# A fill on GpSimd behind each group's gathers, and node inputs loaded at a quad's sums, in a graph attention layer on one Trainium2 core

## The chip, the core and the metric

The kernel runs on 1 core of a Trainium2 chip. A core has a matrix engine (TensorE, PE in the profile; its weight loads are PEld), a vector engine (VectorE, DVE), a scalar engine (ScalarE, ACT), a general engine (GpSimd, POOL) and a sequencer that mostly issues transfers (SyncE, SP). Each takes its own instructions in order; they wait for each other through semaphores. Transfers run on 16 DMA engines.

The metric is device time in microseconds (us). Beside the timed runs, one execution was taken by the hardware profiler; all views of the profile are of that one.

## The reference, cut to what matters

One layer of graph attention over 12500 nodes of 128 features and 200000 edges, sorted by destination. The input is normalised and rectified, projected to 4 heads of 32, scored per edge, put through a softmax over each destination's edges, and summed.

```
h = maximum(layernorm(x), 0)                       # 12500 x 128
hn = (h @ W_node.T).reshape(N, 4, 32)
e  = (edge_attr_64 @ W_edge.T).reshape(E, 4, 32)
att = sum(concat([hn[src], hn[dst], e], -1) * a, -1)     # per edge and head
att = where(att > 0, att, 0.2 * att)
m = maximum(segment_max(att, dst), 0)
ex = exp(att - m[dst])
denom = segment_sum(ex, dst) + (E - deg)[:, None] * exp(-m)
out = x + segment_sum((ex / denom[dst])[:, :, None] * hn[src], dst).reshape(N, 128)
```

The node input `x` is needed twice: at the start, for the projection, and at the end, where it is added to the sums.

## The kernel before, in words

**Tiling.** Edges go in groups of 511 (one more place of the 512 carries the sum of a destination that goes on from the group before). There are 392 groups; 4 groups are a quad (98 quads), and 4 quads, 16 groups, are in most places a "super", the unit of the softmax. Since edges are sorted, a group's destinations lie in a window of at most 92 rows (`SPAN`).

**Stages.** First all nodes are normalised and projected (lines 307 to 448) and written to a table in device memory, 137 numbers a node. Then, for each quad: *logits* (`all_logits`, `open_logits`, `logits`, `add_sources`), for each super the *softmax*, and for each quad the *sums* (`sums`, `complete_group`, `divide`). Sums of one super run beside the logits of the next.

**Gathers.** The rows of the edges' sources are fetched by GpSimd: `gather` (line 132) issues, for each group, four indirect transfers (line 141), 128 rows each, into `ga`. The first 18 groups gather raw rows of `x` before the table is there (72 transfers), the others gather from the table (1494). `ga` has room for 8 quads (`QUADS`). A quad's gathers are issued by `fetch`, which `open_logits(q)` calls for quad q + 2; the first gather of each group waits until PE has summed the group that lay in that place before, eight quads back.

**SyncE's queue.** `open_logits(q)` also issues, for quad q + 2: the edge features `ea` (line 302), the destinations `db` (line 304, waits for a free buffer), and in `fetch_windows` four loads of `pw` (line 502) and four of the node inputs `xw` (line 505, 92 rows of 512 bytes each). A register load on SP precedes each four (`windows`, line 486). Between these stand the stores of the results, four a quad (line 783), which `divide` issues.

**Sums.** For each group DVE weighs the gathered rows (line 736) and makes a matrix of ones and zeros (`hot`, line 749); PE multiplies them for three of the four parts (line 754). The part j = 0 waits for the group before: DVE line 683 and ACT line 687 carry its last row over, PE line 688 multiplies, ACT line 689 copies the sums out (`pt`). A quad's division comes one group later: DVE lines 766 to 776 and the addition of `xw` at line 780 (on GpSimd for a few at the end).

**Order.** The order of instructions on each engine is the program's own: within `tc.manual_schedule()` nothing is reordered, and `together` takes one step of each of its generators in turn. Where a quad's sums and another's logits go together, `sums(q)` comes first, so that its first instructions stand ahead of the loads that `open_logits` issues.

Of the kernel before, what the change touches and what calls it, by code (L numbers as in the profile page):

```python
# [8 lines left out]
F32 = mybir.dt.float32  # L9
# [9 lines left out]
D = H * HD  # L19
# [10 lines left out]
WIN = 96  # L30
SPAN = 92
QG = 4
# [2 lines left out]
SIDE = PIECES * H  # L35
NODE_T = 9
AT_ONCE = 4
RAW, MORE = 4, 2
QUADS = 8
SETS = max(NODE_T, QG * J)  # L40
# [3 lines left out]
def blocks(total, step):  # L44
    return [(i, min(step, total - i)) for i in range(0, total, step)]
# [3 lines left out]
def kernel(  # L49
# [35 lines left out]
    nc = tc.nc  # L85
# [5 lines left out]
    consts = ctx.enter_context(tc.tile_pool(name="consts", bufs=1))  # L91
# [14 lines left out]
                   allow_small_or_imprecise_dtypes=True)  # L106
    ones = consts.tile([P, P], F32, name="ones")
    nc.vector.memset(ones, 1.0)

# [10 lines left out]
    quads = blocks(G, QG)  # L122
# [9 lines left out]
    def gather(q, rows, width, lo, hi):  # L132

        g0, m = quads[q]
        ga = GA[q] = ga_all[:, q % QUADS]
        for i in range(lo, hi):
            n = -(-min(E - (g0 + i) * NE + 1, GE) // P)
            if n < J:
                nc.vector.memset(ga[:, i, n:, :], 0.0)
            for j in range(n):  # L140
                nc.gpsimd.indirect_dma_start(  # L141
                    out=ga[:, i, j, 0:width], out_offset=None, in_=rows,
                    in_offset=bass.IndirectOffsetOnAxis(ap=srci[:, g0 + i, j:j + 1], axis=0))

    def held_gather(q, i, rows, width):

        nc.vector.memset(ga_all[0:1, q % QUADS, i, 0, 0:1], 0.0)
        gather(q, rows, width, i, i + 1)
# [8 lines left out]
    with tc.manual_schedule():  # L157
# [5 lines left out]
        early = [(q, i) for q in range(raw + 1) for i in range(raws(q))]  # L163
        for _ in range(AT_ONCE):
            q, i = early.pop(0)
            gather(q, x, D, i, i + 1)
# [11 lines left out]
        with tc.tile_pool(name="prep", bufs=1) as prep, tc.tile_pool(  # L178
            name="prep_ps", bufs=1, space=bass.MemoryType.PSUM
# [127 lines left out]
        with tc.tile_pool(name="node", bufs=2) as node, tc.tile_pool(  # L307
            name="node_ps", bufs=2, space=bass.MemoryType.PSUM
        ) as node_ps, tc.tile_pool(name="index", bufs=1) as index, tc.tile_pool(
            name="index_ps", bufs=1, space=bass.MemoryType.PSUM  # L310
# [152 lines left out]
    with tc.tile_pool(name="work", bufs=2) as work, \  # L463
            tc.tile_pool(name="turned", bufs=1) as turned, \
            tc.tile_pool(name="ps", bufs=1, space=bass.MemoryType.PSUM) as ps:
        XW, LG, AT, U, DR = {}, {}, {}, {}, {}
# [10 lines left out]
        def groups(s):  # L477
            q0, m = supers[s]
            g0 = quads[q0][0]
            return g0, quads[q0 + m - 1][0] + quads[q0 + m - 1][1] - g0  # L480
# [3 lines left out]
        def windows(of, size, g, n):  # L484

            return nc.values_load_multi_w_load_instructions(
                of[0:1, g:g + n], engines=[mybir.EngineType.SP], min_val=0, max_val=(N - 1) * size,
                skip_runtime_bounds_check_because="a destination's row, and that is a node")[1]
# [7 lines left out]
        def fetch_windows(q):  # L496
            g0, m = quads[q]
            pw = PW[q] = load.tile([SPAN, QG, SIDE], BF16, name="pw")
            xw = XW[q] = work.tile([WIN, QG, D], F32, name="xw", bufs=8)
            at = windows(base_side, 2 * SIDE, g0, m)  # L500
            for i in range(m):
                nc.sync.dma_start(as_bytes(pw[:, i, :]), rows_at(side, at[i], 2 * SIDE))
            at = windows(base_row, 4 * D, g0, m)
            for i in range(m):
                nc.sync.dma_start(as_bytes(xw[0:moved(q), i, :]), rows_at(x, at[i], 4 * D, moved(q)))

        def fetch(q):
            if q not in EA:
                fetch_edges(q)
            fetch_windows(q)  # L510
            if q not in GATHERED:
                GATHERED.add(q)
                gather(q, table, ROW, raws(q), quads[q][1])
# [156 lines left out]
        def complete():  # L670

            division = state.pop("division", None)
            if begun:
                complete_group(*begun.pop())
            if division:
                divide(*division)
# [28 lines left out]
        def marks(q):  # L705

            g0, m = quads[q]
            hot = work.tile([P, QG, J, WIN + 1], F32, name="hot", bufs=3)
            nc.scalar.copy(hot[:, :m, :, WIN], is_last[:, g0:g0 + m, :])  # L709
            if q >= nq - FREE:  # L710
                for i in range(m):
                    for j in range(J):
                        nc.gpsimd.tensor_scalar(hot[:, i, j, 0:WIN], lane, slot[:, g0 + i, j:j + 1],
                                                None, op0=OP.is_equal)
            return hot

        def sums(q):

            g0, m = quads[q]
            s = of_quad[q]  # L720
            s0, sm = groups(s)
            ga = GA.pop(q)
            heads = lambda t: t[:, :, 0:sm * H].rearrange("p j (h g) -> p j h g", h=H)
            ex, xs, facs = XS[s]
            fc = facs[WIN:WIN + 1, 0:sm * H].rearrange("p (h g) -> p h g", h=H)
            pt = work.tile([WIN + 1, QG, ROW], F32, name="pt", bufs=3)
            hot = HOT.pop(q) if q in HOT else marks(q)
            beside = xs[:, :, 0:sm * (H + 1)].rearrange("p j (h g) -> p g j h", g=sm)
            nc.scalar.copy(ga[:, :m, :, R_CNT:R_SRC + H], beside[:, g0 - s0:g0 - s0 + m])

            def weigh(i):

                if i < m:
                    val = ga[:, i, :, 0:H * HW].rearrange("p j (h w) -> p j h w", w=HW)
                    weight = heads(ex)[:, :, :, g0 + i - s0]
                    nc.vector.tensor_tensor(  # L736
                        val, val, weight.unsqueeze(3).to_broadcast([P, J, H, HW]), op=OP.mult)

            ahead = 1 if q >= nq - 2 else 0
            for i in range(ahead):  # L740
                weigh(i)
            for i in range(m):
                g = g0 + i
                if q == nq - 1 - FREE and i == 1:
                    for k in range(FREE):
                        HOT[nq - FREE + k] = marks(nq - FREE + k)
                weigh(i + ahead)
                if q < nq - FREE:
                    nc.vector.tensor_tensor(  # L749
                        hot[:, i, :, 0:WIN], lane_ps.unsqueeze(1).to_broadcast([P, J, WIN]),  # L750
                        slot[:, g, :].unsqueeze(2).to_broadcast([P, J, WIN]), op=OP.is_equal)
                acc = ps.tile([P, 512], F32, name="acc", bufs=3)[0:WIN + 1, 0:ROW]
                for j in range(1, J):
                    nc.tensor.matmul(acc, hot[:, i, j, :], ga[:, i, j, :], start=j == 1, stop=False)  # L754
                complete()
                begun.append((q, i, ga, hot, pt, acc, fc[:, :, g - s0]))
                yield
# [85 lines left out]
        with tc.manual_schedule():  # L843
# [18 lines left out]
            for s, (q0, m) in enumerate(supers):  # L862


                ahead = list(range(q0 + m, sum(supers[s + 1]))) if s + 1 < len(supers) else []
                now, ahead = ahead[:1], ahead[1:]
                beside = [sums(q0 - 1)] if s not in (0, 2) else [] if s else late(2) + [raw_scaled(3)]
                beside += late(raw) if s == 1 else []
                if s == len(supers) - 1:

                    for _ in range(2):
                        next(beside[0])
                if not s:
                    beside.insert(0, some(1, 1, 1, 1, 1, len(held)))
                together(*beside, *map(all_logits, now), softmax(s))
                assert not held
                for k in range(m if s == 1 else m - 1):
                    now, ahead = ahead[:1], ahead[1:]
                    together(sums(q0 + k), *map(all_logits, now), *([] if s else [normed(raw)]))
                    if s > 4:  # L880
                        next(check_steps, None)
                if s < 2:
                    complete()
                for a in ahead:
                    together(all_logits(a))
                if not s:
                    together(*late(3))
            flush()
            together(check_steps)
            last_sums = sums(nq - 1)  # L890
            next(last_sums)
            redo = nc.values_load(flag[0:1, 0:1], min_val=0, max_val=1)
# [200 lines left out]
```

## Time and profile before

| | us |
|---|---|
| median of 3 runs (lowest, highest) | 2575.87 (2572.44, 2578.76) |
| the profiled execution's own time | 2560.06 |
| span of its instructions | 2558.3 |
| GpSimd busy, of it the 1494 table gathers | 1507.2, 1418.7 |
| PE, DVE, ACT busy | 1425.0, 1370.2, 403.5 |
| first table gather, end of the last gather | 136.5, 2436.3 |

The page gives busy time as the union of an engine's instructions; time in which it waits is not in it. The view of the waits adds, for each pair of a waiting line and what ended its wait, the total, the number and the longest; "remote" stands for an increment of a semaphore for which no instruction or transfer was found that ended just before it, and "issue" for time without any wait that the profile shows. A gather's row on POOL is the time of its issue, not that of the transfer. The granted TensorE clock is a share of its full speed; its mean over the span is 0.526.

### The profile page before, as it was taken

The page shows a single profiled execution, that of the slowest core. Times are in us where ns is not written, and L with a number is a line of the kernel's source. Part 1 is how long each engine was busy: PE and PEld are TensorE (multiplying, and loading weights), DVE is VectorE, ACT ScalarE, POOL GpSimd, SP SyncE. Part 2 cuts the span into 40 slices and gives each one's busy share as a digit, 9 for nine tenths or more (in the row PEclk, how much of TensorE's full clock was granted, in tenths as well). Part 3 has the DMA queues.
Part 4 walks back from the last instruction along what each step waited for, and adds up shares of the span by engine and source line. Part 5 has one row for each costly group of instructions (what it writes and reads, how often), then busy time and mean ns, then how long its engine had stood idle before and what let it go on. Part 6 is the DMA issues. An engine that isn't in the chain of part 4 may idle for free. (4 is left out here: it accounts for less than half of the span.)

```text
span 2558.3 us, 27296 instructions
## 1 busy us (share of the span) xinstructions
PE 1425.0 (56%) x7317; PEld 1265.1 (49%) x7317; DVE 1370.2 (54%) x3362; ACT 403.5 (16%) x1531; POOL 1507.2 (59%) x1609
## 2 busy tenths in 40 slices
PE   4555645555555555555555555555655655655486
PEld 3544545544544445445545544544544544544475
DVE  4543545554554555555555555554554554555587
ACT  4533211111111111111111111111111110111112
POOL 6445546566666666566666666666666666666602
PEclk9665655555555555555555555555555555555556
DMA  5433354444445454444444444444444444434330
GB/s 181 153 111 97 99 133 122 109 119 125 113 119 129 108 132 121 106 125 117 117 125 117 116 124 117 116 121 121 116 120 112 123 114 120 123 100 119 94 94 17
DMA packets 195917, 297.27 MB, mean 116 GB/s; under 512 B 70633, under 2 KB 143593, under 8 KB 186354
## 3 DMA queue, kind: packets, MB, share of 16 engines
q1 hardware_dynamic: 143952, 183.30, 26.2%
q0 software_dynamic: 50112, 109.61, 17.4%
q10 hardware_dynamic: 1698, 2.58, 0.3%
q8 instruction: 61, 1.00, 0.2%
q14 instruction: 94, 0.77, 0.1%
HBM read 269.63 MB, written 25.73 MB: 115 GB/s over the span
## 5 line engine op out<-in xcount | busy, mean ns | idle before, releaser
L141 POOL DMA_INDIRECT ga<-table,srci x1494 | 1418.7, 950 | 903.9 <-issue 400.2
L754 PE MATMUL acc<-ga,hot 128*97 128x137 f32 x2352 | 647.6, 447 | 263.6 <-ACT hot L709 100.5
L754 PEld LDWEIGHTS acc<-ga,hot 128*97 128x97 f32 x2352 | 515.9, 278 | 287.3 <-ACT hot L709 101.9
L683 DVE TENSOR_TENSOR ga<-acc,facs 1x132 f32<-1x132 f32 x391 | 115.9, 296 | 710.7 <-ACT pt L689 597.9
L688 PE MATMUL acc<-ga,hot 128*97 128x137 f32 x784 | 267.7, 444 | 361.0 <-ACT ga L687 315.8
L545 PE MATMUL lg<-wblk,ea 128*128 128x8 f32 x1568 | 409.4, 359 | 0.0
L688 PEld LDWEIGHTS acc<-ga,hot 128*97 128x97 f32 x784 | 188.4, 277 | 396.7 <-ACT ga L687 342.3
L545 PEld LDWEIGHTS lg<-wblk,ea 128*128 128x128 f32 x1568 | 381.8, 309 | 0.0
L689 ACT COPY pt<-acc 97x137 f32<-97x137 f32 x392 | 107.1, 273 | 1529.1 <-remote 942.1
L542 PEld LDWEIGHTS <-at 92*128 92x128 bf16 x1568 | 213.9, 165 | 231.5 <-DVE at L536 95.8
L736 DVE TENSOR_TENSOR ga<-ga,ex_ps 128x528 f32<-128x528 f32 x392 | 268.7, 686 | 28.0 <-remote 27.7
L536 DVE TENSOR_TENSOR at<-const_ps,db 92x512 bf16<-92x512 f32 x392 | 267.3, 683 | 5.8
L542 PE MATMUL lg<-pw,at 92*128 92x12 bf16 x1568 | 170.6, 182 | 166.5 <-DVE at L536 80.1
L749 DVE TENSOR_TENSOR hot<-const_ps,slot 128x384 f32<-128x384 f32 x384 | 209.2, 545 | 0.0
L646 PE MATMUL ex_ps<-ident,ex 64*128 64x64 f32 (+2 forms) x112 | 18.6, 315 | 164.0 <-ACT ex L635 99.8
L646 PEld LDWEIGHTS ex_ps<-ident,ex 64*128 64x128 f32 (+2 forms) x112 | 13.8, 208 | 167.1 <-ACT ex L635 102.1
L141 POOL DMA_INDIRECT ga<-in_x_dram,srci x72 | 68.6, 952 | 43.6 <-issue 20.2
L687 ACT COPY ga<-acc 1x1 f32<-1x1 f32 x391 | 59.9, 153 | 189.5 <-DVE ga L683 113.7
L557 DVE TENSOR_REDUCE st<-lg 128x64 f32<-128x192 f32 x98 | 35.0, 357 | 87.9 <-remote 37.6
L395 PE MATMUL row_ps<-wcat,hT 128*128 128x137 f32 x198 | 45.7, 389 | 52.1 <-issue 15.6
L776 DVE TENSOR_TENSOR res<-pt,const_ps 92x512 f32<-92x512 f32 (+3 forms) x102 | 67.5, 662 | 4.4 <-issue 0.6
L780 DVE TENSOR_TENSOR res<-res,xw 92x512 f32<-92x512 f32 (+2 forms) x99 | 67.4, 681 | 3.4
(137 smaller groups left out, 1067.6 us busy)
## 6 DMA issues: line engine op xcount, KB each, us to landing
db<-in_dst_dram SPq DMA_DIRECT2D x98, 768.0 KB
ea<-in_edge_t_dram SPq DMA_DIRECT2D x98, 512.0 KB
ga<-table,srci POOLq DMA_INDIRECT x1494
xw<-in_x_dram SPq DMA_DIRECT2D x384, 46.0 KB
out_dram<-res SPq DMA_DIRECT2D x384, 46.0 KB
pw<-side SPq DMA_DIRECT2D x392, 2.2 KB
table<-row SPq DMA_DIRECT2D x9, 616.5 KB
xt<-in_x_dram SPq DMA_DIRECT2D x9, 576.0 KB
```

The lines of the kernel that those rows point to most:

```text
L141: nc.gpsimd.indirect_dma_start(out=ga[:, i, j, 0:width], out_offset=None, in_=rows, in_offset=bass.IndirectOffsetOnAxis(ap=srci[:, g0 + i, ...
L536: nc.vector.tensor_tensor(at[:, i, :], node_ps[0:SPAN, g0 + i:g0 + i + 1].to_broadcast([SPAN, GE]), db[0:SPAN, i, :], op=OP.is_equal)
L542: nc.tensor.matmul(lg[:, i, j].rearrange("p k h -> p (k h)"), at[:, i, j * P:(j + 1) * P], sw, start=i + j == 0, stop=False, skip_group_ch ...
L545: nc.tensor.matmul(lg[:, i, 2 * w:2 * w + 2, 0, :], ea[:, i, w, :], wblk, start=False, stop=True, skip_group_check=True)
L683: nc.vector.tensor_tensor(ga[0:1, i, 0, 0:H * HW].rearrange("p (h w) -> p h w", w=HW), before[WIN:WIN + 1, 0:H * HW].rearrange("p (h w) -> ...
L688: nc.tensor.matmul(acc, hot[:, i, 0, :], ga[:, i, 0, :], start=False, stop=True)
L689: nc.scalar.copy(pt[:, i, :], acc)
L736: nc.vector.tensor_tensor(val, val, weight.unsqueeze(3).to_broadcast([P, J, H, HW]), op=OP.mult)
L749: nc.vector.tensor_tensor(hot[:, i, :, 0:WIN], lane_ps.unsqueeze(1).to_broadcast([P, J, WIN]), slot[:, g, :].unsqueeze(2).to_broadcast([P, ...
L754: nc.tensor.matmul(acc, hot[:, i, j, :], ga[:, i, j, :], start=j == 1, stop=False)
L776: nc.vector.tensor_tensor(res[:, :n, :].rearrange("p g (h d) -> p g h d", d=HD), val[:, :, :, 0:HD], share_ps[0:R, :n, :].unsqueeze(3).to_ ...
L780: add.tensor_tensor(res[:, :n, :], res[:, :n, :], xw, op=OP.add)
```

## The change

Two edits. In `gather`, behind the four gathers of each group, GpSimd fills `rest`, a tile of one partition and 640 numbers that nothing reads; that makes 392 fills. And the loads of `xw` leave `fetch_windows`, and so the place two quads ahead of a quad's logits; a new function `fetch_inputs(q)` issues them as the first step of `sums(q)`, and `xw` has 3 buffers in place of 8. The register load of line 486 that precedes the four moves along with them.

```
+REST = 640
...
+    rest = consts.tile([1, REST], F32, name="rest")
...
                 nc.gpsimd.indirect_dma_start(
                     out=ga[:, i, j, 0:width], out_offset=None, in_=rows,
                     in_offset=bass.IndirectOffsetOnAxis(ap=srci[:, g0 + i, j:j + 1], axis=0))
+            nc.gpsimd.memset(rest, 0.0)
...
         def fetch_windows(q):
             g0, m = quads[q]
             pw = PW[q] = load.tile([SPAN, QG, SIDE], BF16, name="pw")
-            xw = XW[q] = work.tile([WIN, QG, D], F32, name="xw", bufs=8)
             at = windows(base_side, 2 * SIDE, g0, m)
             for i in range(m):
                 nc.sync.dma_start(as_bytes(pw[:, i, :]), rows_at(side, at[i], 2 * SIDE))
+
+        def fetch_inputs(q):
+            g0, m = quads[q]
+            xw = XW[q] = work.tile([WIN, QG, D], F32, name="xw", bufs=3)
             at = windows(base_row, 4 * D, g0, m)
             for i in range(m):
                 nc.sync.dma_start(as_bytes(xw[0:moved(q), i, :]), rows_at(x, at[i], 4 * D, moved(q)))
...
         def sums(q):
 
+            fetch_inputs(q)
             g0, m = quads[q]
```

On each engine the order of all other instructions stays as it was.

More of the change, by code (lines that the diff above doesn't have):

```diff
@@ L37 @@
 AT_ONCE = 4
+REST = 640
 RAW, MORE = 4, 2
@@ L108 @@
     nc.vector.memset(ones, 1.0)
+    rest = consts.tile([1, REST], F32, name="rest")
     srci = consts.tile([P, G, J], I32, name="srci")
@@ L143, in gather @@
                     in_offset=bass.IndirectOffsetOnAxis(ap=srci[:, g0 + i, j:j + 1], axis=0))
+            nc.gpsimd.memset(rest, 0.0)
     def held_gather(q, i, rows, width):
@@ L498, in fetch_windows @@
             pw = PW[q] = load.tile([SPAN, QG, SIDE], BF16, name="pw")
-            xw = XW[q] = work.tile([WIN, QG, D], F32, name="xw", bufs=8)
             at = windows(base_side, 2 * SIDE, g0, m)
@@ L502, in fetch_windows, with fetch_inputs @@
                 nc.sync.dma_start(as_bytes(pw[:, i, :]), rows_at(side, at[i], 2 * SIDE))
+        def fetch_inputs(q):
+            g0, m = quads[q]
+            xw = XW[q] = work.tile([WIN, QG, D], F32, name="xw", bufs=3)
             at = windows(base_row, 4 * D, g0, m)
@@ L717, in sums @@
         def sums(q):
+            fetch_inputs(q)
             g0, m = quads[q]
```

## The prediction

> **What bounds the kernel now.** I read the busy times first: no engine is above 59%, so a sum of busy times says little. Then the waits, all engines together: the longest two are not for data.
>
> ```profile
> PE 1425.0 (56%) x7317; PEld 1265.1 (49%) x7317; DVE 1370.2 (54%) x3362; ACT 403.5 (16%) x1531; POOL 1507.2 (59%) x1609
> L141 POOL DMA_INDIRECT ga<-table,srci x1494 | 1418.7, 950 | 903.9 <-issue 400.2
> ...
> ACT pt L689 <- remote: 942.1, 105, 12.1
> DVE ga L683 <- ACT pt L689: 597.9, 166, 11.3
> POOL ga L141 <- remote: 260.3, 105, 3.4
> POOL ga L141 <- PE acc L688: 162.9, 36, 23.7
> ```
>
> "Remote" is a semaphore increment that no record explains. ACT line 689 waits for PE's matmul of line 688, and 105 times the increment comes late; DVE, PE and POOL stand behind it. The timeline round one such wait shows it.
>
> ```profile
> 967.07 1.69 PE L754 MATMUL acc<-ga,hot 128*97 128x137 f32 x6
> 967.29 0.94 POOL L141 DMA_INDIRECT ga<-table,srci  x1 [0.30 <-issue]
> 968.54 0.94 POOL L141 DMA_INDIRECT ga<-table,srci  x1 [0.30 <-issue]
> 969.79 0.94 POOL L141 DMA_INDIRECT ga<-table,srci  x1 [0.30 <-issue]
> 973.22 0.27 ACT L689 COPY pt<-acc 97x137 f32<-97x137 f32 x1 [7.81 <-remote]
> 973.45 0.94 POOL L141 DMA_INDIRECT ga<-table,srci  x1 [2.72 <-remote]
> ```
>
> PE's line 688 ended at 966.2, ACT moved at 973.2. In between the trace's semaphore records have one PE increment, at 971.65, and 1.42 us later, from 973.07 on, eight within 0.35 us: the work was done, the news was held, until POOL had issued no gather for 2.3 us. POOL itself waited for that news (a slot of `ga`). So it goes the whole run: POOL issues 12 gathers without a pause (3 groups, 15 us); some 8 us in, PE's increments begin to lag; POOL runs out of free slots, stops, 2.0 to 2.7 us later all increments arrive, and it starts again. That is the pattern of five stops and one longer one in each stretch of 16 groups.
>
> The table by stage is the control: two stretches of 16 groups, then the one after the last gather.
>
> ```profile
> 551.50:648.40 96.90, 53.60 (x276) 47.73 (x276) 51.12 (x116) 11.56 (x51) 60.77 (x65) 0.50 0.46 118
> 2004.40:2101.10 96.70, 53.50 (x275) 47.64 (x276) 50.83 (x116) 11.47 (x51) 60.70 (x64) 0.50 0.46 119
> 2436.30:2500.00 63.70, 50.78 (x273) 46.73 (x274) 56.17 (x131) 13.10 (x52) 0.01 (x1) 0.50 0.32 88
> ```
>
> (Columns: span, then busy us of PE, PEld, DVE, ACT, POOL, granted clock.) The same matmuls (273 to 276) take 96.9 us with gathers running and 63.7 without; the clock is 0.50 in both, and ACT line 689 has no "remote" wait in the last one. So PE and DVE could do a group in 63.7/16 = 4.0 us; POOL needs 4 x (0.950 + 0.304) = 5.02 us; a group takes 96.9/16 = 6.06 us. The bound is the hand-over between the two: POOL stopped by increments that its own gathers hold back.
>
> **The change, part by part.** The sum is made against the profiled execution, 2560.06 us (span 2558.3, 1.8 around it); the median of the runs, 2575.87, is 1.0062 of it.
>
> *The fill.* 392 fills, one behind each group's gathers, 373 of them among the 1494 table gathers. No row has this shape. POOL's own fills are nearest:
>
> ```profile
> masks.py:197 POOL MEMSET ident<- 128x128 f32 x1 | 0.2, 204 | 0.3 <-POOLq L1080 0.3
> L1080 POOL MEMSET const-float32-0.0<- 128x1 f32 x1 | 0.1, 98 | 0.3 <-issue 0.3
> L713 POOL TENSOR_SCALAR hot<-lane,slot 128x96 f32<-128x96 f32 x32 | 17.1, 551 | 69.3 <-issue 64.9 <-PE acc L688 4.5
> ```
>
> (204 - 98)/127 = 0.83 ns an element, so 98 + 639 x 0.83 = 0.63 us (one partition or 128, POOL walks the same 640). It cannot gain POOL time of itself. Lower end: it hides under the 0.30 us that precede every gather, 0.33 us. Upper end: it gets such a gap of its own, 0.94 us, and beside DVE it is lengthened as line 713 was once (0.51 to 0.77), 1.20. Ordinary POOL instructions follow each other with no idle time, so 0.63 is the nearest row; I take 0.78, half a gap more. 373.5 x 0.78 = 291 us of POOL time (0.33: 123; 0.94: 351).
>
> The Trainium skill (SBUF — State Buffer, "SBUF: two separate sides") says GpSimd and VectorE lock a shared port pair for a whole instruction. By it each fill could hold DVE for its length, at most 392 x 0.63 = 247 us. Here the rows differ: beside line 713's 32 instructions DVE's line 736 took 694 ns and line 749 took 548, against 686 and 545 over the run; I count nothing for DVE.
>
> What the fill may take away is the held stretch. Waits of POOL between the first table gather (136.5) and the last (2436.3): 2299.8 - 1494 x 1.254 = 427 us. A pause between gathers was 0.30 us; it becomes 1.08 (0.63 to 1.24). Is that enough for the backlog? How long after POOL's last gather the increments came, by length of the run of gathers that began after a full stop: 16 gathers 2.9 to 3.1 us, 12 about 2.0 to 2.6, 8 about 1.0 to 1.6, the one clear run of 4 1.02. That is some 0.2 us of backlog a gather, about 0.7 to 1.0 after 4. A pause of 1.08 just covers it, 0.63 would not. After the run of 4 at 269.2 POOL stood 1.25 us, and the next run stayed clean for some 7 us, like one after a full stop. I take it that the backlog is gone at most fills, and that a fifth of the waits, 85 us, stays (the longer one where a stretch of 16 groups turns to the next).
>
> New time of the gathers: 1873 + 291 + 85 = 2249, against 2300: -51 us. POOL is then the slower side, at 5.8 us a group against 4.0 for PE and DVE.
>
> Behind the last gather lie 122 us in which 32 groups are still to be summed (122/32 = 3.8 us each). That is many because POOL now fills slots as soon as PE frees them and is eight quads ahead. With POOL the slower, fewer remain: at the least the last two quads with their softmax (8 groups and about 30 us, 61), at the most all 122. I take 85: -37 us. Late next are DVE's additions of line 559, which wait for a quad's gathers.
>
> *The node inputs.* Per quad four loads, four register moves and one register load of SP move from behind the `pw` loads of two quads later to the start of the quad's own sums, ahead of the `ea`, `db` and `pw` loads and behind the four `out` stores of the quad before; POOL's queue is not passed. SP has them on the way in 1.4 to 2 us undisturbed, behind stores of up to 6.6 us; the reader, line 780, comes one group into the next quad, over 17 us after even at 4.0 us a group. With three buffers SP waits for the addition of three quads earlier, which is done. Behind them in SP stand `ea` and `db`, used two quads on. Cost 0, cover at least 8 us; if it failed, DVE would stand at line 780 and with it line 683 and the next group. At the very end the last quad's loads stand behind the stores that wait for POOL's addition (2541.3); they are read at 2548.5. Bounds 0 to 98 x 2 = 196 us should each arrive 2 us late, below nothing by no row; 0 taken.
>
> Sum: 2560 - 51 - 37 = 2472; on the median's scale 2487, rounded to 2485.
>
> **The rivals.** *The pause is too short* (the slower side). Increments lag from 8 us on as now and come free only when POOL runs out of slots. In held time PE gets through a group's six increments in 6 x 1.42 = 8.5 us, otherwise 4.0. A cycle now: 8/4.0 = 2.0 groups, 7/8.5 = 0.8, and 0.2 in the stop make the 3 seen. With 5.80 us a group, n = 2.2 + (5.8n - 8)/8.5, so n = 4.0 and a group takes 5.80 + 2.5/4.0 = 6.42 instead of 5.02 + 0.83 = 5.85: +0.57 x 373.5 = +213, less what the fill saves of the 24 longer stops (5.0 us each): 2653 to 2773, the middle some 2730 on the median's scale. For it: runs that began after a stop of only 1.0 to 1.35 us mostly lagged within 4 us (at 414.9, 1090.5, 2129.4). Against it: those came behind 8 or more gathers. It decides when the backlog of four gathers exceeds the pause; by this arithmetic break-even is an onset at some 17 us instead of 8.
>
> *An even trade*: the fill only takes the place of POOL's idle time, 291 of 427 us, and PE goes on as it does; 2576 on the median's scale. Against it: POOL's stops are what frees PE.
>
> *No backlog at all*: waits 0, fill 0.63, tail 61: 1873 + 235 = 2108, -192 - 61, so 2307 (2321). It is the low end of the forecast's own case.
>
> *Node inputs late*: up to +196, 2770. *The port lock*: DVE idles 46%, so about half of 247, +120, 2610 if the forecast's gain is lost to it as well.
>
> **The numbers.** Forecast's case, with "no backlog" as its edge, 0.58, own range 2375 to 2560; too short 0.32; even trade 0.04; inputs late 0.03; port lock 0.03. 0.3% is 8 us, about what a measurement of this kernel can tell from no change. Faster 0.58, same 0.04, slower 0.38. From 2385 to 2750 leaves out some 6 in 100 below and 12 above.
>
> **What would show it.** Right: a POOL group "rest" of 392 at about 0.63 us; ACT line 689's "remote" down from 105 to under 40; runs of gathers no longer stopped every third group; the delay from line 688 to 689 at 0.04 us most times; waits on "ga" at DVE line 559; PE at about 0.6. Wrong: "remote" near 900 us still, POOL's waits above 300 beside the fills, or DVE idle ahead of line 780. I would be wrong above all if the pause that counts is not 1.08 but nearer 0.63.

## The result and the profile after

The changed kernel took 2542.37 us (median of 10 runs, 2526.88 to 2565.63); the kernel before, on the same chip, 2578.81 (10 runs, 2566.18 to 2586.16). The ratio is 0.985, 95% interval 0.983 to 0.987: 1.5% faster, where the prediction had 3.5% (2485 of 2575.87). All ratios here leave out two slow runs (2565.63 us of the changed kernel, 2395.34 of `rest1040`). The profiled execution took 2542.56 us, its span is 2540.7.

The page of the changed kernel, busy times and groups (columns as before). All lines below have moved by two to seven: 141 is now 143, 688 is 694, 689 is 695, 780 is 787.

```profile
PE 1422.6 (56%) x7317; PEld 1267.3 (50%) x7317; DVE 1369.3 (54%) x3362; ACT 404.5 (16%) x1531; POOL 1756.4 (69%) x2001
...
L143 POOL DMA_INDIRECT ga<-table,srci x1494 | 1425.7, 954 | 650.8 <-issue 382.0
...
L146 POOL MEMSET rest<- 1x640 f32 x392 | 243.5, 621 | 0.1
```

The waits of the changed kernel, all engines (engine, line waited for: us in total, times, longest):

```profile
ACT pt L695 <- remote: 753.6, 104, 10.6
...
DVE st L563 <- remote: 248.3, 42, 9.7
DVE ga L689 <- ACT pt L695: 231.4, 137, 8.0
...
POOL ga L143 <- PE acc L694: 103.9, 27, 22.9
...
POOL ga L143 <- remote: 69.5, 49, 1.9
```

POOL has 249 us more work and stands less. But the held increments are still there: ACT at line 695 waits 754 us for them in place of 942, as often as before (104 times), and DVE now waits 248 us for them at line 563 (38 before, as line 557). The timeline of the changed kernel shows one round (start, length, instruction, the idle time ahead of it and what ended it):

```profile
861.50 1.31 POOL L143 DMA_INDIRECT ga<-table,srci  x1 [0.30 <-issue]
862.29 0.66 PE L694 MATMUL acc<-ga,hot 128*97 128x137 f32 x2
863.11 0.94 POOL L143 DMA_INDIRECT ga<-table,srci  x1 [0.30 <-issue]
864.04 0.62 POOL L146 MEMSET rest<- 1x640 f32 x1
864.82 0.95 POOL L143 DMA_INDIRECT ga<-table,srci  x1 [0.16 <-issue]
866.08 0.94 POOL L143 DMA_INDIRECT ga<-table,srci  x1 [0.30 <-issue]
866.58 0.27 ACT L695 COPY pt<-acc 97x137 f32<-97x137 f32 x1 [5.72 <-remote]
...
868.73 0.66 PE L694 MATMUL acc<-ga,hot 128*97 128x137 f32 x2
...
874.99 0.62 POOL L146 MEMSET rest<- 1x640 f32 x1
876.72 0.27 ACT L695 COPY pt<-acc 97x137 f32<-97x137 f32 x1 [9.35 <-remote]
```

PE ended line 694 at 862.95 and ACT moved at 866.58, 3.6 us late; the next time at 869.39 and 876.72, 7.3 us late, after POOL had run out of slots. The fill starts as the gather ends, and the next gather 0.16 us after the fill, not 0.30. So a group's fill adds 0.621 + 0.159 - 0.305 = 0.475 us. POOL now stops mostly after 16 gathers (58 of 118 runs of gathers between waits of over 0.9 us; 12 gathers only 29 times), where before it was 12 (107 of 152).

The table by stage, 16 groups with gathers running and then without (span, then busy us of PE, PEld, DVE, ACT, POOL, granted clock):

```profile
542.40:638.00 95.60, 56.10 (x286) 50.04 (x287) 51.96 (x121) 11.87 (x52) 72.11 (x82) 0.50 0.46 118
2418.40:2482.00 63.60, 49.85 (x273) 45.52 (x273) 55.73 (x130) 13.38 (x53) 0.59 (x1) 0.55 0.30 80
```

That is 95.6 in place of 96.9 us, and the stage without gathers is as it was. Over the whole: the first table gather starts at 136.9 (136.5 before), the last ends at 2418.4 (2436.3), and 122.3 us follow, with 30.4 groups still to be summed (122.0 and 30.3). The 18 us are gained among the gathers alone: 1494 x 1.254 = 1873 of gathers, 177 of fills, and 231 of waits where there had been 427.

One more figure is used below, ACT's lag: while table gathers run, the time that ACT's line 689 (695 now) stood behind the end of PE's line 688 (694) of the same group, summed over the groups in which this was over 0.4 us. It was 891 us before (152 of 361 groups) and is 811 after (167 of 360). It is not the same as "remote": the view puts an increment that comes late down to a PE matmul when one happens to have ended shortly before, and a steady lag is then counted only in part. The fill took waits from POOL and gave PE's successors little.

### The profile page after: what moved, and what is told of

Same layout as the page of the kernel before. It is cut to its first block, busy times and chain, and to the rows that moved or that the text cites. A ratio compares the mean times of both kernels' runs of the same rounds, so it can differ in the third digit from the quotient of the medians.

```text
span 2540.7 us, 27705 instructions
## 1 busy us (share of the span) xinstructions
PE 1422.6 (56%) x7317; PEld 1267.3 (50%) x7317; DVE 1369.3 (54%) x3362; ACT 404.5 (16%) x1531; POOL 1756.4 (69%) x2001
## 5 line engine op out<-in xcount | busy, mean ns | idle before, releaser
L146 POOL MEMSET rest<- 1x640 f32 x392 | 243.5, 621 | 0.1
```

Source lines behind the costliest of these rows:

```text
L146: nc.gpsimd.memset(rest, 0.0)
```

## The experiments

What was to be told apart: that a pause behind each group clears the backlog if it is long enough (the prediction's own case); that what counts is the mean distance from one gather to the next; that the gathers' bytes are what holds the increments; and which of the two edits acts. Ratios are to the kernel before on the same chip. The distance of a kernel is (4 gathers + their fills + 0.16 us behind each fill + 0.30 us ahead of each other gather) / 4, from its own rows; it is 1.25 us before and 1.38 after.

### Which edit acts

`inputs_only`, the moved loads without the fill:

```
-    rest = consts.tile([1, REST], F32, name="rest")
...
-            nc.gpsimd.memset(rest, 0.0)
```

> The changed kernel without the fill: node inputs loaded at the sums, 3 buffers. Theory A (the pause behind the gathers frees PE's held increments, the loads are hidden): ratio to before 1.000, between 0.997 and 1.003, runs of 12 gathers as before. Theory B (the gain is that of the moved loads, the fill only replaces idle time): ratio 0.985, as with both edits.

2557.39 us, ratio 0.9999 (0.9985 to 1.0012). Its waits:

```profile
ACT pt L693 <- remote: 899.9, 103, 12.1
DVE ga L687 <- ACT pt L693: 532.7, 149, 11.2
```

Alone the moved loads cost nothing and bring nothing, so the 1.5% is put down to the fill. The fill without the moved loads was not tried.

### How long the fill is

Each is the changed kernel with one number changed:

```
-REST = 640
+REST = 320        (rest320; 900, 1040, 1120 and 1280 likewise)
```

> The changed kernel with 320 elements in each fill: about 0.36 us, so a pause of some 0.52 us instead of 0.78 and 0.21 us of POOL time a group. Theory A (gain grows with the pause until POOL's own time is the bound): ratio to before 0.990 to 0.997, between none and 640. Theory B (moved loads): 0.985. Theory C (the gain is a lucky phase of POOL against the rest): anything, above 1 too.

> The changed kernel with 1280 elements: fill 1.15 us, pause 1.30 us, 6.00 us of POOL time a group. Theory A with a backlog of about 1 us behind four gathers: the pause now covers it, ACT's waits for late increments fall from 754 us to under 250, gathers end about 40 us earlier than with 640 and the ratio to before is 0.960 to 0.975. Theory D (PE's increments are held at a rate that the pause hardly changes; POOL follows PE at 6.1 us a group): ratio 0.980 to 0.995, late increments stay above 600 us.

> 900 elements: fill 0.85 us, pause 1.00 us, 5.70 us a group, 1.42 us a gather. If a gather needs 1.41 us or less of whatever holds PE's increments, none are late: span near 112 + 2129 + 43 = 2284, ratio 0.895. If it needs more (up to the 1.50 that 1280 allowed), they are late again and the ratio lies between 0.95 and 0.985.

> 1040 elements: fill 0.96 us, pause 1.12 us, 5.81 us of POOL time a group, 1.45 us a gather in the mean. Theory A1 (four gathers leave about 1 us of backlog, a pause longer than that clears it each time): no late increments, as with 1280; first table gather near 113, 373.5 x 5.81 = 2170, tail 43, so a span near 2330 and a ratio near 0.911. Theory A2 (the pause must reach some 1.3 us): late increments come back, ratio 0.94 to 0.98.

| elements | fill, us | added a group, us | distance, us | ACT's "remote", us | ACT's lag, us | ratio (95%) |
|---|---|---|---|---|---|---|
| none (`inputs_only`) | | 0 | 1.25 | 900 | 879 | 1.000 (0.9985-1.0012) |
| 320 | 0.355 | 0.21 | 1.31 | 823 | 806 | 1.000 (0.9985-1.0016) |
| 640 (the change) | 0.621 | 0.475 | 1.38 | 754 | 811 | 0.985 (0.983-0.987) |
| 900 | 0.837 | 0.69 | 1.43 | 547 | 896 | 0.973 (0.969-0.976) |
| 1040 | 0.955 | 0.81 | 1.46 | 340 | 535 | 0.927 (0.920-0.933) |
| 1280 | 1.156 | 1.01 | 1.51 | 0 | 0 | 0.940 (0.938-0.942) |

("Added" is the fill + 0.159 - 0.305. The rows come from three chips, on which the kernel before took 2578.8, then 2556.5 for none, 320 and 1280, and 2557.2 for 900 and 1040.)

A fill of 320 is paid in full by the waits that it replaces. The gain is small up to 900 and large between 900 and 1040. It is not spread over the run. In the middle 64 gathers, 16 groups, take 96.7 us before, 95.8 with 640 elements, 93.3 with 900 and 93.2 with 1040 (medians over all stretches of 64): with 900 the lag is as long as ever, yet the middle is as fast as with 1040. Of the 125 us between the spans of these two, 22 lie ahead of the first table gather, 26 in the first 128 table gathers and 64 behind the last one. The waits of the kernel with 1280 elements:

```profile
PEld L548 <- DVE at L542: 831.9, 168, 12.7
PE lg L548 <- DVE at L542: 761.5, 161, 12.3
DVE U L565 <- DMA ga<-table,srci: 759.7, 85, 13.4
ACT pt L695 <- PE acc L694: 507.8, 276, 4.7
POOL ga L143 <- issue: 412.5, 1517, 0.3
```

No wait there ends "remote". The longest real wait is DVE's for a quad's gathers, and PE waits behind DVE: POOL's work is now the bound, with gathers from 112.6 to 2363.1, which is 2250.5 us for 1494 gathers or 1.506 each. All that lies behind the last gather, as a stage:

```profile
2363.10:2406.00 42.90, 22.41 (x110) 18.12 (x110) 26.11 (x79) 8.98 (x36) 19.48 (x36) 0.66 0.11 29
```

The ratio of 0.940 is below the 0.960 to 0.975 that was expected. In the middle 64 gathers take 96.4 us, hardly less than before (96.7): there the fills have taken the place of POOL's waits. The gain is elsewhere: 43 us behind the last gather in place of 122, since POOL is no longer eight quads ahead; 24 us ahead of the first table gather; and the first 128 table gathers take 193 us in place of 237.

### How the pauses are spread

`rest_each160`, `rest_each300` and `rest_each320` fill behind each gather, not behind each fourth; `rest_quad` puts four fills of 1280 behind every fourth group:

```
                     in_offset=bass.IndirectOffsetOnAxis(ap=srci[:, g0 + i, j:j + 1], axis=0))
-            nc.gpsimd.memset(rest, 0.0)
+                nc.gpsimd.memset(rest, 0.0)      (rest_each..., REST = 160, 300, 320)
...
+            for _ in range(4 if (g0 + i) % QG == QG - 1 else 0):      (rest_quad, REST = 1280)
+                nc.gpsimd.memset(rest, 0.0)
```

> The same 640 elements in four fills of 160, one behind each gather: about 0.23 us each, pauses of 0.39 us. Theory A by total pause: POOL time a group up by some 0.33 us, ratio to before 0.985 to 0.993. Theory A with a pause that must be long in one piece: no gain, 0.997 to 1.005, and runs of gathers stop every third group as before.

> Four fills of 320 behind single gathers, together 1280 elements: pauses of 0.51 us, 5.84 us of POOL time a group, 1.46 us a gather. Theory A by mean rate (a gather needs a certain time of a shared path, between 1.37 and 1.50 us): late increments gone or nearly, span near 112 + 2181 + 43 = 2336, ratio 0.91 to 0.93. Theory A with one long pause needed: late increments stay above 500 us, ratio 0.98 to 1.02.

> Four fills of 1280 in a row behind each fourth group, none behind the other three: the POOL time of 1280 behind each (6.0 us a group), with 16 gathers in a row and then some 4.8 us of pause. Theory A by backlog: increments are late from about the 7th gather to 3 us into the pause, so about half the time; ratio 0.97 to 1.00. If only the mean rate counted: 0.94 as with one fill behind each group.

> Four fills of 300, one behind each gather: pauses of 0.49 us, about 5.77 us a group, 1.44 us a gather. By mean rate between 900 elements (1.42, late) and 1040 (1.45, mostly not): late increments between 200 and 500 us, ratio 0.920 to 0.945.

| | distance, us | ACT's "remote", us | ACT's lag, us | ratio (95%) | before on its chip |
|---|---|---|---|---|---|
| `rest_each160` | 1.33 | 764 | 756 | 0.992 (0.989-0.994) | 2556.5 |
| `rest_each300` | 1.45 | 717 | 875 | 0.978 (0.976-0.981) | 2576.4 |
| `rest_each320` | 1.47 | 158 | 238 | 0.926 (0.921-0.931) | 2557.2 |
| `rest_quad` | 1.54 | 1031 | 1001 | 1.024 (1.021-1.027) | 2557.2 |

Four short fills and one long one give the same time at nearly the same distance (1.47 beside 1.46: 0.926 and 0.927). One pause of some 5 us behind 16 gathers does not, though its mean distance is the largest of all. It is slower than before, where at worst no change was expected. The timeline of `rest_quad` says why:

```profile
1004.18 0.27 ACT L696 COPY pt<-acc 97x137 f32<-97x137 f32 x1 [0.86 <-PE acc L695]
1004.43 0.95 POOL L143 DMA_INDIRECT ga<-table,srci  x1 [0.17 <-issue]
...
1015.58 0.27 ACT L696 COPY pt<-acc 97x137 f32<-97x137 f32 x1 [4.51 <-PE ex_ps L615]
...
1024.29 4.79 POOL L147 MEMSET rest<- 1x1280 f32 x4
1027.38 0.27 ACT L696 COPY pt<-acc 97x137 f32<-97x137 f32 x1 [10.87 <-remote]
```

Sixteen gathers come 1.25 us apart, 20 us in a row; within them PE's increments fall behind as ever, and ACT stands 10.9 us until 3.1 us into the pause. So the distance has to hold over a short stretch: holding it over four gathers (6 us) is enough, over sixteen (25 us with the pause) it is not. The lag begins some 8 us into a run, which fits; no length between was tried.

`rest_each300` was a miss: at 1.45 us it should have been near `rest1040`, and was nearer 900. It ran, with the next two, on a chip on which the kernel before is 0.8% slower.

### Whether it is the bytes

`narrow` is `inputs_only` with gathers that, from the ninth quad on, fetch the last 32 of a row's 137 numbers:

```
-                    out=ga[:, i, j, 0:width], out_offset=None, in_=rows,
+                    out=ga[:, i, j, 0:width] if q < QUADS else ga[:, i, j, 105:width], out_offset=None,
+                    in_=rows,
```

> No fill (as inputs_only); the gathers of all quads from the ninth on fetch 32 numbers of a row (128 bytes) instead of 137 (548 bytes), the same rows in the same number of transfers; the other 105 numbers of a row stay what the place held, so the result is another one. Theory M1 (what holds PE's increments back is the moving of the gathered bytes): late increments nearly gone, POOL's own 5.02 us a group the bound, span near 112 + 373.5 x 5.02 + 45 = 2030, ratio 0.79 to 0.85. Theory M2 (it is the making and handling of a gather's row entries, whatever their size): waits of ACT for late increments stay near 900 us, ratio 0.98 to 1.00.

2574.47 us, ratio 1.0000 (0.9984 to 1.0017). Its waits:

```profile
ACT pt L694 <- remote: 926.6, 113, 12.3
DVE ga L688 <- ACT pt L694: 489.8, 154, 9.2
...
POOL ga L142 <- remote: 255.0, 110, 3.8
```

ACT's lag is 927 us. With 128 bytes a row in place of 548 nothing changes, though the gathers' queue keeps the DMA engines busy half as long, as the pages of before and of `narrow` have it:

```profile
q0 software_dynamic: 50112, 109.61, 17.4%
q0 software_dynamic: 50112, 32.31, 8.5%
```

So neither the bytes nor the time of moving them holds the increments. What stays the same is the number: gathers, rows, and 32 packets a gather, of which 16 carry 4 bytes. None of these was varied, so which of them counts is open.

### One chip for all

On the chip of `narrow` 1120 elements did worse than 1040 had done elsewhere:

> 1120 elements: fill 1.02 us, pause 1.18 us, 5.87 us a group. The share of late increments falls on from 340 us with 1040 (to 50 to 200), POOL is the bound: span near 110 + 373.5 x 5.88 + 48 = 2354, ratio 0.920 to 0.930. If late increments were not what separates 1040 from 1280, it would lie on the line between 0.9267 and 0.9399, at 0.931.

2459.21 us, ratio 0.954 (0.952 to 0.955), 503 us of "remote" at ACT's line 695. That is only half of its lag, which is 999 us, over 0.4 us in 322 of 362 groups:

```profile
1004.41 0.78 PE L694 MATMUL acc<-ga,hot 128*97 128x137 f32 x2 [1.02 <-issue]
1007.97 0.28 ACT L695 COPY pt<-acc 97x137 f32<-97x137 f32 x1 [3.61 <-PE acc L761]
1008.81 0.78 PE L694 MATMUL acc<-ga,hot 128*97 128x137 f32 x2 [1.10 <-ACT pt L695]
1013.76 0.27 ACT L695 COPY pt<-acc 97x137 f32<-97x137 f32 x1 [5.00 <-remote]
```

ACT moves 2.8 us after line 694 has ended, then 4.2 us; the view calls only the second "remote". A longer distance with more held increments fits a mean distance as the cause only if chips differ. So 1040, 1120, 1280 and 320 behind each gather were run again together, on another chip (before: 2556.67):

> The kernel after with 1040 elements in each fill, once more, beside 1120, 1280 and four fills of 320 a group, all on one chip. Theory A (a rate: the increments are on time once the gathers come some 1.45 us apart or slower; the path's rate differs a little between chips): as 1120 was 0.954 on one chip and 1040 was 0.927 on another, the order of 1040 and 1120 must turn round on one chip: where 1040 keeps late increments, 1120 has fewer and is faster. Here 1040 gives 0.925 to 0.965. Rival B (the length of the fill against the order of the engines' work matters, not the rate): 1040 is again the faster of the two on one chip, by 2% or more, with fewer late increments than 1120.

> 1120 elements in each fill, once more. Theory A: faster than 1040 of the same chip or within 0.5% of it, with less time in the waits of ACT that end remote; 0.915 to 0.955. Rival B: slower than 1040 by 2% or more, near 0.954 again.

> 1280 elements in each fill, once more. Both theories: no late increments, 0.940 within 0.005, since the gathers themselves then set the time; what it tells is how far this holds on another chip. If the path's rate is lower on this chip by more than 3%, late increments would appear here too, and the ratio would be above 0.945.

> 320 elements behind each gather, once more. Theory A: it stands by 1040 and 1120 as its mean distance of gathers does (1.46 us, between theirs), so between their ratios or within 0.01 of one of them. Rival B: even pauses work better than one a group, so it is faster than both by more than 0.01.

| | distance, us | ACT's "remote", us | ACT's lag, us | gathers, us | after the last gather, us | us | ratio (95%) |
|---|---|---|---|---|---|---|---|
| 1040 | 1.46 | 480 | 775 | 2195.0 | 81.7 | 2380.34 | 0.930 (0.928-0.933) |
| 320 behind each | 1.47 | 114 | 191 | 2200.0 | 42.0 | 2362.61 | 0.926 (0.923-0.928) |
| 1120 | 1.47 | 65 | 100 | 2202.5 | 43.5 | 2356.24 | 0.922 (0.920-0.923) |
| 1280 | 1.51 | 0 | 1 | 2250.1 | 42.7 | 2406.45 | 0.942 (0.940-0.943) |

In order of distance now: the held increments fall steadily, and the time is least where they are nearly gone and the fill is not yet longer than it need be. The timeline of 1120 elements on this chip:

```profile
1001.35 0.66 PE L694 MATMUL acc<-ga,hot 128*97 128x137 f32 x2
1001.53 1.02 POOL L146 MEMSET rest<- 1x1120 f32 x1
1002.05 0.27 ACT L695 COPY pt<-acc 97x137 f32<-97x137 f32 x1 [1.72 <-PE acc L761]
1002.71 0.94 POOL L143 DMA_INDIRECT ga<-table,srci  x1 [0.16 <-issue]
...
1005.78 0.66 PE L694 MATMUL acc<-ga,hot 128*97 128x137 f32 x2
1006.45 0.94 POOL L143 DMA_INDIRECT ga<-table,srci  x1 [0.30 <-issue]
1006.48 0.27 ACT L695 COPY pt<-acc 97x137 f32<-97x137 f32 x1 [1.72 <-PE acc L761]
```

ACT follows PE's line 694 by 0.04 us while POOL gathers without a stop. Its span is 202.8 us below that of the profile of before: 97.3 between the first and the last table gather (45 of it in the first 128), 78.5 behind them, 27.1 ahead of them.

So the chips do differ: the same 1120 elements leave a lag of 100 us on one and of 999 on another, while gather and fill take the same time on both (949 and 1023 ns, 948 and 1021 ns). Each chip was used in one session, so chip and session cannot be told apart. The 640 elements of the change ran where the kernel before took about as long as on the chip of `narrow` (2578.8 and 2576.4 us), so that row of the first table may belong to a chip of that kind. 1280 elements ran on two chips, at 0.940 and 0.942, without a "remote" wait on either. 1120 is the fastest kernel here (2356 us), 1280 the one with a margin; both beat the changed kernel. Whether 1280 is enough on a chip like that of `narrow` was not tried.

## Why the prediction was right or wrong

**The bound** was read rightly. Where gathers come slowly enough (1280 elements), "remote" and POOL's waits go to 0, and the kernel is 6% faster with the same matmuls; with 1120 on the one chip, the lag down to 100 us, 8%.

**The fill's duration** was right (0.63 us from the rows, 0.621 measured), what it adds was not: 0.78 us forecast, 0.475 measured. Half a gap more was allowed for it; in fact it has no gap, and the next gather's is halved. In the sum, 177 us in place of 291.

**The step that failed** is "A pause of 1.08 just covers it, 0.63 would not." The backlog of "some 0.2 us of backlog a gather" had been read from gathers 1.25 us apart, with their gaps of 0.30 in it. Against it stands only what the fill adds to that, not the whole pause: 0.475 us (0.78 by the forecast's own price) against 4 x 0.2 = 0.8, not 1.08. The 0.30 was counted twice. The runs bear this out: with 900 elements the whole pause is 1.00 us, above 0.8, and ACT's lag is 896 us, as before; only what it adds, 0.69, is below. The figure 0.2 itself holds on two chips: 1.254 + 0.2 is a distance of 1.45 us, and between 1.43 and 1.47 the lag fell from 896 to 238 us on one, and from 775 to 100 between 1.46 and 1.47 on the other. Added 0.81 (1040 elements) cleared a part on both, 0.88 (1120) nearly all on the second; on the chip of `narrow` 0.88 cleared none. The warning "if the pause that counts is not 1.08 but nearer 0.63" is what came: it was 0.78, of it 0.475 new.

**The waits left** follow from that: 231 us in place of "a fifth of the waits, 85 us". Against the sum of 2472 that is +146, the shorter fill -114, together +32 among the gathers.

**The tail** was forecast at 85 us and stayed at 122: "With POOL the slower, fewer remain" had a condition that was not met, as POOL still ran out of slots (its 32 groups left were 30.3 before and 30.4 after). That is +37. 2472 + 32 + 37 = 2541; the profiled execution took 2542.56. Where the condition was met, the tail was 42 to 44 us, shorter than the 61 given as the least.

**The rivals.** "The pause is too short" is what happened, in its mechanism: lag from some 8 us on, release when POOL runs out of slots, runs of four groups. Its price was wrong in sign. By its own formula with 0.475 us in place of 0.78, 5.49 us a group make n = 3.6, and 5.49 + 2.5/3.6 = 6.18 us a group; measured were 2281.4/373.5 = 6.11. The 5.85 that it was set against leaves out the longer stops (24 x 5.0 = 120 us, 0.32 a group); with them before's own waits, 427 us over 373.5 groups, make 5.02 + 1.14 = 6.16. So with the fill at its measured size the rival's price was near nothing, up to +0.33 x 373.5 = +123 us if no longer stop were saved, and the time ended on the faster side. (Against 6.16 its break-even, by the same formula, is an onset at some 15 us, not 17.) "No backlog at all" (2321) was out of reach of 640 elements; 1120 came to 2356. "Node inputs late": no; `inputs_only` is at 1.000. "An even trade" describes a fill of 320 elements.

"The port lock" did not come: DVE's two lines of `ga` and `hot` took 686 and 545 ns before and, as lines 743 and 756, 686 and 545 after, beside 392 fills. But these lines read one of their two inputs from PSUM, and the Trainium skill (SBUF — State Buffer, "SBUF: two separate sides", under "Who interferes with whom") has a narrower sentence than the one weighed: a VectorE instruction with two inputs in SBUF contends with a GpSimd instruction that reads SBUF, "not with one that only writes it". A fill only writes, and the trace agrees: line 787 adds two tiles in SBUF, and took 687 ns in the 14 cases of 92x512 numbers that overlapped a fill, 688 in the other 81 (with 1280 elements 687 in 86 cases, 693 in 9).

**What was to show it.** Right: 392 fills at about 0.63. Not so: "remote" is 754 us and 104 times, not under 40, PE is at 56%, not 60, and the delay from line 694 to 695 is at 0.04 us in 189 of 360 groups, no more than before (199 of 361). In between: POOL's waits 231 us.

What inside the chip the gathers and PE's increments share is not seen in any trace. Shown is that it goes with how closely the gathers follow each other, not with their bytes, and that it nearly keeps up at some 1.47 us a gather on two chips, wholly at 1.51 on two, and not at 1.47 on the chip of `narrow`.

## What to carry to other kernels

When an engine's semaphore increments come late ("remote") beside back-to-back indirect gathers, look at the distance from one gather to the next, over a few gathers: slowing the gathers by a sixth, with work that nobody reads, took 8% off this kernel on one chip. Measure the lag from the end of the very instruction that is waited for: the name that a view of waits gives to a late increment can be that of another. See also in which part of the run a gain lies: here most of it lay at the start and the end, not in the steady middle. A remedy that has a threshold is worth little below it (0 and 1.5% at 320 and 640 elements, 7 to 8% at 1040 to 1120 on two chips, 4.6% on a third), so measure three sizes and not one, and leave a margin for other chips. When a pause is compared with a backlog, count only what it adds to the gaps that were there while the backlog grew.

## What the runs showed of the hardware

- A GpSimd fill on one partition took 0.221, 0.355, 0.621, 0.837, 0.955 and 1.156 us for 160, 320, 640, 900, 1040 and 1280 elements: 0.83 us per 1000 and some 0.09. It starts as the gather ahead of it ends, and the gather behind it starts 0.16 us after it, where one gather follows another after 0.30.
- On two chips ACT's lag behind PE fell to 100 to 240 us, from some 890, once gathers came about 1.47 us apart on average over four; at 1.25 the increments fall back by some 0.2 us a gather. 128 or 548 bytes a row made no difference.
- Chips differ in this: 100 and 999 us of lag at the same instruction times, and the kernel before takes 2557 us on three chips and 2576 to 2579 where the change itself and where `narrow` ran.
